# Half-slot order, PSUM banks and layer norms in a four-layer graph network

## The chip, the cores and the metric

The kernel runs on one core of a Trainium2 chip. The metric is the device time of one execution in microseconds (us); lower is better. A core has five engines with instruction streams of their own: TensorE (PE, matmuls; PEld is its weight load), VectorE (DVE), ScalarE (ACT), GpSimd (POOL) and SyncE (SP, which here only issues DMAs). Each engine works its stream in order. They wait for each other through semaphores.

## The reference

Sixteen graphs of 1,024 nodes with 128 features pass through four layers; after each stands a residual sum and a layer norm.

```python
x = layernorm(x + att(x, adj))         # 0: relu(q) relu(k)^T, masked softmax, times v
x = layernorm(x + edge_max(x, adj))    # 1: max over neighbours j of relu(p[i] + q[j] + b)
x = layernorm(x + mlp(x, adj))         # 2: (x + adj^T x) W1, relu, W2
x = layernorm(x + sage3(x, dilate(adj)))  # 3: three convolutions on a thinned adjacency
```

Two parts set the shape of the kernel. Layer 1 takes for each node and each of 128 features a maximum over its neighbours. And `dilate` walks the rows of the adjacency one after the other: in each row with more than ten neighbours some are removed, a removal at (n, m) also removes (m, n), and so earlier rows change what later rows see.

```python
def step(carry, n):
    row = jnp.take(carry, n, axis=0)
    num = jnp.sum(row)
    sf = jnp.where(num > 10, (num + 1) // 2, 1)
    rm = row & (cumsum(row) % sf == 0)    # and only where num > 1
    carry = carry.at[n].set(row & ~rm)
    carry = carry.at[:, n].set(carry[:, n] & ~rm)
```

## The kernel before

**Layer 1 by lookups.** The nodes of a graph are cut into 86 groups of 12, each of two sixes. For every six, `tables_of` (line 447) makes the maximum of q over each of its 64 subsets on VectorE. The neighbours of a node within a six name one subset. So a maximum over neighbours is a lookup by group, written as a matmul with a one-hot matrix, and a running maximum over the 86 groups. One group of one graph is a **slot**; there are 16 x 86 = 1,376 slots. For slot s:

- `count(s, h)` (line 686), two slots ahead: a matmul of the group's adjacency columns with the table `lit` gives `pm` in PSUM, and ScalarE's Relu makes of it the one-hot `hot` (lines 693, 694), for each half h of the 1,024 nodes.
- `table(s)` (line 696), every second slot: two transposes bring the subset table of two groups into PSUM (`pt`), ScalarE copies it to `high` (line 707), and `low_part` (line 710) has VectorE take the difference `low` (line 713), so that two rounded products give the full precision.
- `look_up(s, h, pg)` (line 716): four row-packed matmuls into the two banks of a tile `pg` (line 722).
- the maximum of `best` and `pg` on VectorE (line 782; in a graph's first slot a copy, line 780).

**The other layers as streams.** Everything else is put between these steps. Generators (`scores`, `attend`, `rest`, `tables_of`) yield one piece at a time through `ask` (line 248): its engine, a cost in us, whether it takes or gives back a PSUM bank, a delay in slots since the stream's last piece, and an event that must have happened. `advance(engines)` (line 667) walks through the streams and emits each piece whose engine still has room. The room grows by a fixed amount each slot (`ROOM`, line 660). It is a plan made while the program is written out: no time is measured in it, and the engines then keep the order. `attend` (line 352) is the softmax and the product with v of layer 0 for the next graph; `scores` (line 289) makes q, k, v and the scores, and after layer 0 its q and p for layer 1; `rest` (line 382) finishes layer 1 of the graph before and does layer 2. `columns_of` (line 269) transposes a graph's rows, `product_of` (line 278) multiplies, each into a bank from `shared` (line 251).

**A slot** (`slot`, line 734) writes out: `low_part` in odd slots; pieces on PE, then pieces on ACT, DVE and POOL; both counts of slot s + 2; both lookups; pieces on PE again; due steps of the dilation; in even slots the table; the first maximum; pieces on ACT, DVE and POOL; the second maximum.

**PSUM** has eight banks. `pg` takes two tiles of two banks, `pm` two banks (tag `subset`), the pieces of the streams one (tag `shared`), tables and the dilation's counts one (tag `tables`).

**The layer norms** of layers 0 to 2 are `norm` (line 261): eight `bn_stats` on VectorE, then `norm_rows` (line 206) on GpSimd: ten small operations for mean and factor, and eight `tensor_scalar` that apply them (line 222).

**The dilation** (`dilation`, line 477) runs through 32 blocks of 32 rows, all 16 graphs at once, as one more generator that yields (slots until the next step, VectorE cost, whether the next step wants a bank). A block has 43 slots: a matmul counts each row's remaining neighbours (`pc`, line 553), VectorE copies them (`low_counts`, `rest`, lines 556 to 558); GpSimd walks the 31 rows within the block, eleven small operations a row in a chain (lines 571 to 581), and notes the hits; those go through DRAM and back in another layout (lines 585 to 589); then VectorE takes them out (`hit_T`, line 592) and does the bulk: for each of four groups q two scans (`rank`, line 618), ScalarE's absolute value (line 621), the comparison `gone` (line 624), and a transpose for later blocks (`last_T`, line 629). The results go to DRAM through SP's queue (`removed`, `removed_T`). At the start of the next block the last of them is taken out of its rows and counted (lines 545 to 558).

Ahead of the slots the first graph's attention is computed alone; after them `rest` of the last graph, the last step of the dilation, and layer 3.

Of the kernel before, what the change touches and what calls it, by code (L numbers as in the profile page):

```python
# [29 lines left out]
F32 = mybir.dt.float32  # L30
# [41 lines left out]
def tile_graph_layers(ctx: ExitStack, tc, a, out):  # L72
# [133 lines left out]
    def norm_rows(dst, src, st):  # L206

        mv = small.tile([P, 4, T], F32, name="ln_mv")
        mean, apart, var, rs = (mv[:, i, :] for i in range(4))
        gp = nc.gpsimd  # L210
        gp.tensor_add(mean, st[:, :, 1], st[:, :, 4])
        gp.tensor_sub(apart, st[:, :, 1], st[:, :, 4])
        gp.tensor_scalar(mean, mean, -0.5, 0.0, op0=ALU.mult, op1=ALU.add)
        gp.tensor_mul(apart, apart, apart)
        gp.tensor_add(var, st[:, :, 2], st[:, :, 5])
        gp.tensor_scalar(var, var, 1.0 / D, LN_EPS, op0=ALU.mult, op1=ALU.add)
        gp.tensor_scalar(apart, apart, 0.25, 0.0, op0=ALU.mult, op1=ALU.add)
        gp.tensor_add(var, var, apart)
        gp.tensor_tensor(rs, var, mhalf, op=ALU.pow)
        gp.tensor_mul(mean, mean, rs)  # L220
        for t in range(T):
            gp.tensor_scalar(dst[:, t, :], src[:, t, :], rs[:, t:t + 1], mean[:, t:t + 1],
                             op0=ALU.mult, op1=ALU.add)
# [6 lines left out]
    def layers_012():  # L230
# [15 lines left out]
        happened, streams, made, planned = {}, [], [], False  # L246
# [4 lines left out]
        def shared(name):  # L251
            if planned:
                return psum.tile([P, 512], F32, tag="shared", name=name, bufs=1)
            return psum.tile([P, 512], F32, tag="subset", name=name, bufs=2)

        def tables_bank(name):

            return psum.tile([P, 512], F32, tag="tables", name=name, bufs=1)


        def norm(dst, src):
            st = small.tile([P, T, 6], F32, name="ln_st")
            for t in range(T):
                yield ask("V", 0.29, same=True)
                nc.vector.bn_stats(out=st[:, t, :], in_=src[:, t, :])
            yield ask("Pool", 0)
            norm_rows(dst, src, st)
# [21 lines left out]
        def scores(b):  # L289
# [48 lines left out]
            yield ask("A", 0.01, after=("X1", b), delay=5)  # L338
# [43 lines left out]
        def rest(b):  # L382
# [16 lines left out]
            yield from columns_of(xT, X[b], first=5)  # L399
            left = w4.tile([P, T, D], F32, name="left", tag="y")  # L400
            parts = w4.tile([P, 3, T, D], BF, name="parts")
            for k in range(3):
                yield ask("A", 1.05)
                nc.scalar.copy(parts[:, k], left if k else X[b])
                if k < 2:
                    yield ask("V", 1.22)
                    nc.vector.tensor_sub(left, left if k else X[b], parts[:, k])
# [69 lines left out]
        def dilation():  # L477
# [59 lines left out]
            now, last_T = load(0), None  # L537
            for _ in prepare(0, *now):
                pass
            for k in range(K):  # L540
                E, V, _, counts = now
# [8 lines left out]
                p = tables_bank("pc")  # L550
                for c, slots in enumerate(((0, 2, 3), (1, 4))):
                    for i in slots:
                        nc.tensor.matmul(p[:B, c * R:(c + 1) * R], spread[:, i].rearrange("p q g -> p (q g)"), of_row,
                                         start=(i == slots[0]), stop=(i == slots[-1]))
                low = dil.tile([B, R], F32, name="low_counts")
                nc.vector.tensor_copy(low, p[:B, 0:R])
                rest = dil.tile([B, R], F32, name="rest")
                nc.vector.scalar_tensor_tensor(rest, p[:B, R:2 * R], 0.5, half_mask[:, own], op0=ALU.add, op1=ALU.mult)  # L558
                if k + 1 < K:
# [4 lines left out]
                for n in range(R - 1):  # L564
# [17 lines left out]
                    yield 0.95, 0.06, False  # L582
# [7 lines left out]
                yield B * NP / K - 37.75, 0, False  # L590
# [24 lines left out]
                for q in range(Q):  # L615
                    rank = dil.tile([P, N], F32, name="rank", bufs=2)
                    for h, s in enumerate(halves):
                        nc.vector.tensor_tensor_scan(rank[:, s], E[:, q, s], E[:, q, s], rank[:, 511:512] if h else 0.0,  # L618
                                                     op0=ALU.add, op1=ALU.max)
                        yield 0.34, 1.2, False  # L620
                    nc.scalar.activation(rank, rank, AF.Abs, bias=centre[:, q:q + 1], scale=scale[:, q:q + 1])  # L621
                    yield 0.34, 0, False
                    gone = dil.tile([P, N], BF, name="gone", bufs=2)
                    nc.vector.scalar_tensor_tensor(gone, rank, width[:, q:q + 1], E[:, q, :],  # L624
                                                   op0=ALU.is_equal, op1=ALU.mult)
                    nc.sync.dma_start(out=removed[k, :, q, :], in_=gone)
                    yield 0.34, 1.3, False
                    if after:
                        nc.vector.transpose(last_T[:, q].rearrange("p k r -> p (k r)"), gone[:, (k + 1) * R:])
                        if after > 1:  # L630
                            nc.sync.dma_start(out=removed_T[k + 2:, :, q, own].rearrange("k p r -> p k r"),
                                              in_=last_T[:, q, 1:, :])
                    yield 0.34, 0.8, q == Q - 1
                if after:
                    now = following
# [19 lines left out]
        now, bank_free = 0, 0  # L655
# [10 lines left out]

        def advance(engines):
            nonlocal bank_free
            for stream in list(streams):
                while True:  # L670
# [5 lines left out]
                    if (engine not in engines or now < at + delay or room[engine] <= 0 and give is False or (take and now < bank_free)  # L676
                            or after and now <= happened.get(after, now) or third and now % 3):
                        break
                    room[engine] -= cost
                    if take:  # L680
                        bank_free = 1 << 30
                    if give:
                        bank_free = now + 0.5
# [12 lines left out]
        def table(s):  # L696
# [4 lines left out]
            pt = tables_bank("pt")[:, :2 * P]  # L701
# [32 lines left out]
        def slot(s, last):  # L734
# [19 lines left out]
            advance(("PE",))  # L754
            advance(("A", "V", "Pool"))
            ahead = s + 2 if s + 2 < last else None
            if ahead is not None:
                for h in range(2):
                    count(ahead, h)
            pgs = []  # L760
            if s >= 0:
                for h in range(2):
                    pgs.append(psum.tile([P, 2, 512], F32, tag="wide", name="pg", bufs=2))
                    look_up(s, h, pgs[h])
                hots.pop(s)
            now = s + 0.5
            advance(("PE",))
            if s >= 0:
                while due <= s and (s % 2 or not wants_bank):
                    after, cost, wants_bank = next(dilate, (B * NP, 0, False))  # L770
                    due += after
                    room["V"] -= cost
            if ahead is not None and ahead % 2 == 0:
                table(ahead)
            for h, pg in enumerate(pgs):
                if h:
                    advance(("A", "V", "Pool"))
                own = bests[b][:, :, halves[h]]
                if g == 0:
                    nc.vector.tensor_copy(own, pg)  # L780
                else:
                    nc.vector.tensor_max(own, own, pg)  # L782

        dilate = dilation()
        due, wants_bank = 0.0, True
# [16 lines left out]
        with tc.manual_schedule(engines={mybir.EngineType.PE, mybir.EngineType.Activation, mybir.EngineType.DVE,  # L802
                                         mybir.EngineType.Pool}):
            planned = True
# [3 lines left out]
            planned = False  # L808
# [312 lines left out]
```

## Time and profile before

| what | value |
|---|---|
| median of three runs | 7495.03 us (7492.15 to 7495.25) |
| span of the profiled execution | 7491.3 us |
| mean granted clock of TensorE | 0.844 |
| busy: PE, DVE, ACT, POOL | 5627.2, 5493.4, 3343.2, 3585.3 us |
| slots, from the first maximum to the last | 132.3 to 6166.1 us |
| maximum at line 782 | 2,720 times, 1,211 ns each |
| `hot` at line 694 | 2,752 times, 686 ns each |
| norm applied on GpSimd, line 222 | 384 times in layers 0 to 2, 450 ns each |
| subtraction `left`, line 407 | 32 times, about 1.22 us each |

The profile is one execution, recorded by the hardware. A "busy" time is the sum of the instructions of an engine; matmuls are pipelined[...], so a busy PE is not PE at its peak. A wait names the engine and line that waited, and whose end released it. A window is a stretch of the span in us from its start. Durations in the prediction are means of such rows.

### The profile page before, as it was taken

To read this page: it belongs to the slowest core of one execution; us is meant where nothing else is said; L and a number is where in the kernel's file an instruction comes from. 1 tells how busy PE (TensorE), PEld (TensorE's weight loads), DVE (VectorE), ACT (ScalarE), POOL (GpSimd) and SP (SyncE) were. 2 spreads that over 40 slices of the span, in tenths; PEclk is the share of its full clock that TensorE was granted. 3 is DMA by queue.
4 is the path that set the end of the run, shared out by engine and by line. 5 is a ranking of instruction groups with operands and counts; after the bars stand their busy time and mean duration, and the time that the engine had idled before them with its cause. 6 is when DMAs were issued, how large, how long until landed. Compare 5 with 4: busy or idle time off the path is not lost.

```text
span 7491.3 us, 84114 instructions
## 1 busy us (share of the span) xinstructions
PE 5627.2 (75%) x26430; PEld 2905.1 (39%) x26554; DVE 5493.4 (73%) x8459; ACT 3343.2 (45%) x5465; POOL 3585.3 (48%) x11637
## 2 busy tenths in 40 slices
PE   6768687878787777676767676777777767778996
PEld 3334243434343434343334343433343324555653
DVE  3788787878788878787878777878787883444453
ACT  3445454445454545454444444445444432333751
POOL 3454555555555555555554555555555541110116
PEclk8889787878787979787878788888888778888998
DMA  5121212121212121212121202121111106665544
GB/s 34 18 24 18 29 18 29 18 29 18 28 18 29 19 29 19 28 18 29 18 29 18 28 14 28 15 28 18 28 16 21 22 18 112 113 113 110 186 161 152
DMA packets 494372, 318.87 MB, mean 43 GB/s; under 512 B 316650, under 2 KB 445668, under 8 KB 489828
## 3 DMA queue, kind: packets, MB, share of 16 engines
q0 software_dynamic: 105648, 84.20, 12.9%
q1 hardware_dynamic: 383600, 228.10, 10.7%
q8 instruction: 209, 3.42, 0.2%
q10 hardware_dynamic: 4676, 1.19, 0.1%
q14 instruction: 239, 1.96, 0.1%
HBM read 413.70 MB, written 118.16 MB: 71 GB/s over the span
## 4 chain that ended last, share of the span: by engine, by line
DVE 30%; PE 29%; POOL 22%; issue 8%; ACT 6%; DMA 4%; SPq 0%; another core or an unknown queue 0%; DVEq 0%; ACTq 0%; POOLq 0%
DVE best L782 13%; PE pg L722 7%; PE pagg L901 5%; DVE rank L618 3%; PE pav L373 3%; POOL sc L576 2%; PE pm L693 2%; DVE sub L463 2%; POOL hit L578 2%; DVE gone L624 2%; POOL sc L571 2%; POOL last_rank L579 2%; POOL sc L573 2%; PE pe L363 2%; PE psc L325 2%
## 5 line engine op out<-in xcount | busy, mean ns | idle before, releaser
L782 DVE TENSOR_TENSOR best<-best,pg 128x1024 f32<-128x1024 f32 x2720 | 3207.4, 1211 | 704.6 <-PE pg L722 701.5
L694 ACT ACTIVATE hot<-pm,one_less 128x512 fp32r<-128x512 f32 x2752 | 1739.2, 686 | 1059.5 <-PE pm L693 1056.4
L722 PE MATMUL pg<-hot,high 64*128 64x512 f32 x5504 | 1485.8, 536 | 911.6 <-DVE best L782 888.4
L722 PEld LDWEIGHTS pg<-hot,high 64*128 64x128 f32 x5504 | 583.5, 208 | 2068.7 <-DVE best L782 1595.5
L722 PE MATMUL pg<-hot,low 64*128 64x512 f32 x5504 | 1229.0, 442 | 0.0
L693 PE MATMUL pm<-AT,lit 120*128 120x512 fp8e4 x2752 | 955.9, 431 | 13.2 <-ACT hot L694 6.0
L487 POOL DMA_DIRECT2D E<-in_adj_dram x128 | 70.3, 558 | 1844.2 <-issue 1028.4
L707 ACT CAST high<-pt 128x256 fp32r<-128x256 f32 x688 | 255.1, 371 | 935.0 <-PE pt L705 933.1
L722 PEld LDWEIGHTS pg<-hot,low 64*128 64x128 f32 x5504 | 612.1, 218 | 30.8
L571 POOL TENSOR_SCALAR sc<-low_counts,half_mask,rest 16x1 f32<-16x1 f32 x992 | 341.3, 344 | 287.7 <-DVE rest L558 191.1
L576 POOL TENSOR_SCALAR sc<-sc 16x1 f32<-16x1 f32 x992 | 394.6, 398 | 104.4
L693 PEld LDWEIGHTS <-lit 120*128 120x128 fp8e4 x2752 | 271.1, 107 | 323.8 <-issue 260.3
L573 POOL TENSOR_SCALAR sc<-sc 16x1 f32<-16x1 f32 x992 | 331.8, 334 | 107.2
L621 ACT ACTIVATE rank<-rank,centre,scale 128x1024 f32<-128x1024 f32 x128 | 158.6, 1239 | 502.0 <-DVE rank L618 502.0
L373 PE MATMUL pav<-v,eT 128*128 128x128 f32 x2048 | 330.7, 317 | 52.4 <-ACT eT L366 52.3
L325 PE MATMUL psc<-kT,qT 128*128 128x512 f32 x512 | 291.9, 653 | 83.5 <-DVE y L377 48.5
L578 POOL TENSOR_SCALAR hit<-V,sc 16x31 bf16<-16x31 bf16 (+30 forms) x992 | 354.5, 357 | 0.0
L931 POOL TENSOR_TENSOR length<-length,mhalf 128x8 f32<-128x8 f32 x48 | 79.0, 1645 | 570.3 <-DVE length L930 570.3
L579 POOL TENSOR_SCALAR last_rank<-V,sc 16x31 f32<-16x31 bf16 (+30 forms) x992 | 344.4, 347 | 0.0
L373 PEld LDWEIGHTS pav<-v,eT 128*128 128x128 f32 x2048 | 290.5, 222 | 124.7 <-ACT eT L366 75.9
L705 PE MATMUL pt<-ident,sub 128*128 128x128 f32 x1376 | 322.0, 320 | 1.7
L363 PE MATMUL pe<-ident,e 128*128 128x128 f32 x1024 | 212.0, 344 | 146.9 <-ACT e L335 88.7
(242 smaller groups left out, 9213.5 us busy)
## 6 DMA issues: line engine op xcount, KB each, us to landing
removed<-gone SPq DMA_DIRECT2D x128, 256.0 KB
An<-in_adj_dram POOLq DMA_DIRECT2D x16, 1024.0 KB, 15.8
E<-in_adj_dram POOLq DMA_DIRECT2D x128, 128.0 KB, 6.4
gone_all<-removed POOLq DMA_DIRECT2D x64, 256.0 KB, 12.1
near<-in_adjT_dram POOLq DMA_DIRECT2D x16, 1024.0 KB, 17.3
h<-x SPq DMA_DIRECT2D x32, 512.0 KB
kept<-near SPq DMA_DIRECT2D x16, 1024.0 KB
share<-share SPq DMA_DIRECT2D x32, 512.0 KB
```

The costliest lines, as they stand in the source:

```text
L325: nc.tensor.matmul(psc, qT[:, t * P:(t + 1) * P], kT[:, s], start=True, stop=False)
L373: nc.tensor.matmul(pav, eT[:, c, :], values[b][:, c, :], start=(c == 0), stop=(c == T - 1))
L571: gp.tensor_scalar(half, mine, half_mask[:, m], rest[:, n:n + 1], op0=ALU.mult, op1=ALU.add)
L573: gp.tensor_scalar(sf, half, 5.5, sf, op0=ALU.is_gt, op1=ALU.mult)
L576: gp.tensor_scalar(to, at, sf, none, op0=ALU.subtract, op1=ALU.subtract)
L578: gp.tensor_scalar(hit[:, n, n + 1:], V[:, n, n + 1:], at, None, op0=ALU.is_equal)
L579: gp.tensor_scalar(last[:, n + 1:], V[:, n, n + 1:], to, None, op0=ALU.is_le)
L693: nc.tensor.matmul(pm, lit[:, r, :], AT[b * (T + 1) + c][:, halves[h]], start=True, stop=True)
L694: nc.scalar.activation(hots[s][:, halves[h]], pm, AF.Relu, bias=one_less)
L722: nc.tensor.matmul(pg[:, a], part[rows, at * P:(at + 1) * P], hots[s][rows, halves[h]], start=(k == 0), stop=(k == 1))
L782: nc.vector.tensor_max(own, own, pg)
L901: nc.tensor.matmul(pa[:, s], piece[:, c, :], m[c][:, s], start=(c == 0 and k == 0), stop=(c == T - 1 and k == 1))
```

## The change

- In each half slot the lookup now stands first, then the pieces (PE, then the others). The dilation's steps come in the first half, the two counts and the table in the second, and each half ends with its maximum.
- `shared` has two banks, and `advance` keeps account of which piece holds which. The tag `tables` is gone: tables take turns with the counts on the two `subset` banks, and the dilation's counts take a bank of `shared` through `hold`.
- `norm_rows` is split: `norm_factors` stays on GpSimd; for layers 0 to 2 the eight applications become ScalarE activations, asked for four slots after GpSimd's part. The last norm, of layer 3, still uses `norm_rows` on GpSimd.
- The two subtractions `left` in `rest` go from VectorE to GpSimd, and ScalarE's copies after them are asked for 2.5 slots later.
- Two delays of five slots (transposes after a norm) become half a slot.
- In the dilation the scans of group q stand ahead of the comparison of group q - 1, `low_counts` and `rest` are a step of their own after the counts' matmul, and the slots of a block are divided anew: rows every 0.90 in place of 0.95, 7.34 in place of 5.25 for the way through DRAM, steps of the bulk every 0.36 in place of 0.34.

```diff
     def norm_rows(dst, src, st):
+        rs, mean = norm_factors(st)
+        for t in range(T):
+            nc.gpsimd.tensor_scalar(dst[:, t, :], src[:, t, :], rs[:, t:t + 1], mean[:, t:t + 1],
+                                    op0=ALU.mult, op1=ALU.add)
+
+    def norm_factors(st):
...
-        for t in range(T):
-            gp.tensor_scalar(dst[:, t, :], src[:, t, :], rs[:, t:t + 1], mean[:, t:t + 1],
-                             op0=ALU.mult, op1=ALU.add)
+        return rs, mean
...
         def shared(name):
-            if planned:
-                return psum.tile([P, 512], F32, tag="shared", name=name, bufs=1)
-            return psum.tile([P, 512], F32, tag="subset", name=name, bufs=2)
+            return psum.tile([P, 512], F32, tag="shared", name=name, bufs=2)
...
             yield ask("Pool", 0)
-            norm_rows(dst, src, st)
+            rs, mean = norm_factors(st)
+            for t in range(T):
+                yield ask("A", 0.25, same=(t > 0), delay=4)
+                nc.scalar.activation(dst[:, t, :], src[:, t, :], AF.Identity, bias=mean[:, t:t + 1],
+                                     scale=rs[:, t:t + 1])
...
-            yield ask("A", 0.01, after=("X1", b), delay=5)
+            yield ask("A", 0.01, after=("X1", b), delay=0.5)
...
-            yield from columns_of(xT, X[b], first=5)
+            yield from columns_of(xT, X[b])
...
-                yield ask("A", 1.05)
+                yield ask("A", 1.05, delay=2.5 if k else 0.5)
                 nc.scalar.copy(parts[:, k], left if k else X[b])
                 if k < 2:
-                    yield ask("V", 1.22)
-                    nc.vector.tensor_sub(left, left if k else X[b], parts[:, k])
+                    yield ask("Pool", 0)
+                    nc.gpsimd.tensor_sub(left, left if k else X[b], parts[:, k])
...
-                p = tables_bank("pc")
+                yield 0, 0.3, True
+                p = shared("pc")
+                own_bank = hold()
...
+                yield 0.5, 0.2, False
                 low = dil.tile([B, R], F32, name="low_counts")
...
-                    yield 0.95, 0.06, False
+                    yield 0.9, 0.06, False
...
-                yield B * NP / K - 37.75, 0, False
+                yield B * NP / K - 35.66, 0, False
...
+                for q in range(Q + 1):
+                    if q < Q:
+                        rank = ranks[q] = dil.tile([P, N], F32, name="rank", bufs=2)
...
+                    if q:
+                        gone = dil.tile([P, N], BF, name="gone", bufs=2)
...
...
-            pt = tables_bank("pt")[:, :2 * P]
+            pt = psum.tile([P, 512], F32, tag="subset", name="pt", bufs=2)[:, :2 * P]
...
+            for h in range(2):
+                now = s + 0.5 * h
+                if s >= 0:
+                    pg = psum.tile([P, 2, 512], F32, tag="wide", name="pg", bufs=2)
+                    look_up(s, h, pg)
+                advance(("PE",))
+                advance(("A", "V", "Pool"))
+                if h == 0:
+                    while s >= 0 and due <= s and not (wants_bank and taken >= 2 and given.get(taken - 2, 1e9) > now):
+                        after, cost, wants_bank = next(dilate, (B * NP, 0, False))
+                        due += after
+                        room["V"] -= cost
+                elif s + 2 < last:
+                    for half in range(2):
+                        count(s + 2, half)
+                    if s % 2 == 0:
+                        table(s + 2)
+                if s >= 0:
+                    own = bests[b][:, :, halves[h]]
...
```

## The prediction

> **What bounds the kernel now.** First the page's busy shares: no engine is full (PE 75%, DVE 73%, ACT 45%, POOL 48%), so the time lies in waits between engines. Then the view by line: the maximum at line 782 (2,752 with its 32 copies at line 780, two per slot) starts at 132.3 us and ends at 6166.1 us. That is 1,376 slots of 4.385 us, 86 slots (about 381 us in the middle) a graph, and all that the change touches, but for a few steps before and after.
>
> Then the waits, us in total, times, longest:
>
> ```profile
> DVE best L782 <- PE pg L722: 701.5, 340, 18.0
> PE pg L722 <- DVE best L782: 888.4, 989, 26.0
> ACT xT L276 <- POOL X L222: 228.2, 16, 19.8
> DVE hit_T L592 <- DMA hit_p<-hit: 129.7, 16, 23.5
> DVE gone L624 <- ACT rank L621: 77.9, 46, 3.5
> DVE low_counts L556 <- PE pc L553: 56.3, 30, 3.6
> ```
>
> The reader is to see that VectorE waits for lookups and TensorE for VectorE, in turn. Sixteen times, once a graph, PE and ACT stand still for a layer norm that GpSimd has not applied; sixteen times VectorE waits for the dilation's result.
>
> A graph holds two dilation blocks (43 slots each), so I cut one graph at the dilation's own marks: from its row counts (line 558) to VectorE's first step on the result (line 592), the "window" in which GpSimd walks 31 rows; and from there to the next counts, the "bulk". The view by stretches (length; busy us of PE, PEld, DVE, ACT, POOL with instructions; clock; DMA):
>
> ```profile
> 2400.80:2542.40 141.60, 113.76 (x570) 59.81 (x575) 113.47 (x179) 75.66 (x131) 95.92 (x332) 0.92 0.07 7
> 2542.40:2587.00 44.60, 30.06 (x148) 14.82 (x147) 39.96 (x56) 19.24 (x29) 1.83 (x4) 0.89 0.20 41
> 2587.00:2724.20 137.20, 107.51 (x533) 51.04 (x532) 107.18 (x162) 65.95 (x119) 105.60 (x356) 0.90 0.20 23
> 2724.20:2776.20 52.00, 30.51 (x108) 13.22 (x108) 47.19 (x67) 16.70 (x25) 2.32 (x5) 0.51 0.36 53
> ```
>
> The two bulks are VectorE's (40 of 44.6, 47 of 52.0). In the first window nobody is full: GpSimd's rows end at 2517.2, 25 us before the result is used, and VectorE idles 28 us. The second window ends on GpSimd: rows end at 2712.3, the DMA lands, VectorE has waited 7.9 us. So the windows have different limits: coupling in the first, GpSimd's chain in the second.
>
> **What the Trainium skill says.** "TensorE: Matmul & The Clock Gate" (Part 1, What's actually happening): the clock is half or full, by recent activity. The trace agrees: 0.51 in the second bulk, about 0.9 in the windows. I assume the same clock after; 0.05 more or less is 6% of PE's 282 us, 17 us a graph, perhaps half of it on the path. "Perfetto Trace Analysis" (Optimization Strategy): repeated bubbles can mean too few PSUM buffers. Here one bank serves all of the other layers' pieces, and all eight are in use (4 lookups, 2 counts, 1 tables, 1 pieces). "PSUM — Partial Sum Buffer" (bank collisions): guard by bank, so a table written into a counts bank must wait until ScalarE has read that bank; no trace of before has this wait.
>
> **The change, part by part.** Sums are per graph.
>
> 1. *Order in the half slot.* Before, PE does pieces, counts, both lookups, pieces, table; VectorE gets nothing new between one slot's second lookup and the next slot's first. After, one lookup opens each half slot. Nothing is added: 8 lookup matmuls and 2 maxima a slot as before. What can be won is VectorE's 701.5/16 = 44 us, less about 11 that belong to the stall in 2.
>
> 2. *Norms applied on ScalarE, four slots after GpSimd's factors.* GpSimd loses 3 x 8 x 0.45 = 10.8 us (line 222): 3.5 in the first window, 7 in the second (bn_stats of one and two norms lie there in the changed order). ScalarE gains 24 instructions. "ScalarE: Activation LUTs" (What ACT_TABLE_LOAD costs) gives 280 ns + 0.833 ns an element with one pointer operand, 93 for a second, 93 overlapped: about 0.39 us, 9.4 us a graph. The rank activation (two pointers, 1,024 elements) took 1,239 ns, formula 1,226. ScalarE has room, busy 177.6 of 375.4. The new waits: behind a norm on ACT stand the `hot` activations, two slots ahead of the lookups, so some 6 us late are covered. The 228.2 us wait goes.
>
> 3. *The two subtractions of line 407 go to GpSimd*: VectorE loses 2 x 1.22 = 2.4 us. No row shows such a subtraction there; "GPSIMD Engine Reference" (Elementwise) has 4,497 ns for 2,048 elements, so I estimate 2.25 us for 1,024. Bounds: 1.2 (VectorE's) to 4.5. In the changed order the first falls into the bulk, where GpSimd is idle, the second at the start of the second window's rows: +2.25 there.
>
> 4. *Two banks for pieces; tables share the two counts banks.* Gain: a piece no longer waits for the last eviction (in the waits `psc <- y`, 48.5 us in all; small). Cost: in each even slot the order is count, count, table on two banks, so the table's transposes wait for the first `hot`. One such place, before:
>
> ```profile
> 2268.22 0.60 PE L693 MATMUL pm<-AT,lit 120*128 120x512 fp8e4 x2
> 2268.65 1.27 ACT L694 ACTIVATE hot<-pm,one_less 128x512 fp32r<-128x512 f32 x2 [0.40 <-PE pm L693]
> ```
>
> The first hot ends 0.43 + 0.69 = 1.1 us after the counts start; the counts occupy PE for 0.45. PE waits 0.65 us if ScalarE is free, about 1.2 if an eviction (0.59) stands before it, 0 where VectorE is behind anyway. I take 0.65 for 43 tables: 28 us, some 12 in each window. Behind the table on PE stands the next lookup, and VectorE behind that.
>
> 5. *Dilation.* Scan of row group q before gone of q-1 hides ScalarE's rank: 77.9/16 = 4.9 us off, in the bulks. Counts are read a slot after their matmul: 56.3/16 = 3.5 off as a wait, given back as a later start. The writes of `gone` and `last_T` on SP's queue move along, some 2.5 us later for each of the first three; they are read a block later, and the next that VectorE waits for on SP, the result's, is a window away. The counts' matmul now takes a pieces bank, so it stands behind an eviction of at most 0.7 us. By the changed order the slots are, first window, bulk, second window, bulk: 34.0, 8.0, 35.7, 8.3 before, 36.0, 6.6, 36.3, 7.1 after. A slot's two maxima (2.35 us back to back) move with them.
>
> *Sum.* First window: PE 113.8 + two more slots (3.8 at full clock) + 12 for tables + 3.4 of today's waits on ACT's results = 133; VectorE 113.5 + 4.7 - 2.4 = 116, with half of its 28 us idle 130; GpSimd 112.9 + about 11 for the DMA = 124. I take 133. Second window: GpSimd 137.2 - 7 + 2.25 = 132.4 stands above VectorE (109 busy) and PE (107.5 + 5 moved in + 12); I take 133: the stall and the wait on the result go only as far as that chain. Bulks: 40.0 - 1.4 x 2.35 + 1.8 = 38.5; 47.2 - 1.2 x 2.35 + 4.1 = 48.5. Together 353 against 375.4, 6.0% less. Fifteen graphs (132 to 5843 us) lose 0.06 x 5711 = 341 us; the last, where VectorE waits for GpSimd already (23.5 us), about 5; outside the slots a norm and two subtractions change engines, +1. Span 7491.3 - 345 = 7146; the runs' median is 3.7 above the span: **7150 us**.
>
> **The rivals.**
>
> - *Coupling vanishes.* GpSimd bounds both windows (124, 132.4), bulks at VectorE's 37 and 45: 338, ten per cent less, 7495 - 570 = about 6930. For: VectorE is busy for 308 of 375 us only. Against: the table's wait.
> - *Only small gain.* The table's wait eats the first window's gain (141), the second is GpSimd's (134), bulks 41 and 50: 366, or 2.5% less: about 7340. For: PE busy 114 of 141.6 leaves 28 us for all waits.
> - *Slower: tables wait behind ScalarE.* PE is busy 282 us a graph; its other waits, 93.5 less 52 for VectorE's maxima, are 41.5. 375.4 - 282 - 41.5 = 52 us is all that 43 tables may cost: from 1.2 us each PE sets a longer graph. ScalarE's pieces (0.6 to 1.35 us) and bursts of norms stand before `hot` in the same half slot. At 1.5 us: +13 a graph, +206: 7700. Against: not every half slot has a piece, and part of the 41.5 goes with item 1.
> - *The change does nothing*: the order is written out by hand, so it does move instructions; only an exact offset gives this.
>
> **How the numbers follow.** Forecast (7010 to 7240) 0.53; coupling vanishes 0.13; small gain 0.25; slower 0.07; no difference 0.02. Range 6990 to 7340: it leaves out most of the first rival, the last two and a little of the second. A measurement of this kernel tells about 0.2% from no change. Faster by more than 0.2%: 0.91; within: 0.02; slower: 0.07.
>
> **What would show it.** Right: the wait of `xT` on GpSimd's X is gone, `best <- pg` falls from 701.5 to some 400, `gone <- rank` below 20; `hit_T` keeps a wait in the second windows; a new wait of `pt` on `hot`, some 0.65 us each; first windows near 133 us, second near 133. Wrong: first windows still 141 (the table's wait is larger), second windows well under 132 (rows got faster), a clock that moved by over 0.05, or `hot` waiting for GpSimd's factors on ACT.

## The result, and the profile after

| | median us | runs | ratio to before, 95% interval |
|---|---|---|---|
| before | 7495.14 | 4, 7492.15 to 7509.31 | |
| after | 7411.32 | 4, 7408.36 to 7422.13 | 0.9887 [0.987, 0.9904] |

The change makes the kernel 1.1% faster. The forecast was 4.6%; the time lies 71 us above the range's upper end.

The page of the kernel after gives busy time and share by engine, and the shares of the chain that ended last:

```profile
PE 5789.6 (78%) x26554; PEld 2790.6 (38%) x26554; DVE 5516.8 (74%) x8427; ACT 3510.6 (47%) x5849; POOL 3475.9 (47%) x11285
...
PE 48%; DVE 31%; ACT 10%; issue 5%; POOL 4%; DMA 2%; ACTq 0%; DVEq 0%; SPq 0%; POOLq 0%
```

The chain of the kernel before:

```profile
DVE 30%; PE 29%; POOL 22%; issue 8%; ACT 6%; DMA 4%; SPq 0%; another core or an unknown queue 0%; DVEq 0%; ACTq 0%; POOLq 0%
```

GpSimd has all but left the path, but PE and ScalarE took its place. The view of waits says at what (us in total, times, longest):

```profile
PE pg L737 <- DVE best L791: 609.5, 685, 11.0
...
PE pt L720 <- ACT hot L709: 463.7, 655, 5.1
...
DVE low L728 <- ACT high L722: 364.6, 364, 7.0
...
DVE best L791 <- PE pg L737: 255.5, 293, 4.2
...
DVE e L330 <- PE psc L328: 172.0, 161, 15.4
...
DVE y L379 <- PE pav L375: 122.2, 98, 5.1
```

Three of these waits, in the kernel before:

```profile
DVE y L377 <- PE pav L373: 57.5, 60, 5.5
...
DVE e L328 <- PE psc L326: 43.5, 49, 15.3
...
DVE low L713 <- ACT high L707: 33.7, 51, 6.0
```

Here `e` and `y` are VectorE's steps on the scores and on the product with v. VectorE's wait for lookups fell from 701.5 to 255.5 us, and PE's wait for the maxima from 888.4 to 609.5. The stall of `xT` on X, 228.2, is no longer in the list. New are 464 us in which PE stands before a table; the wait of VectorE for that table's copy grew from 34 to 365.

The same graph as in the prediction, cut at the same marks, in the view by stretches (length; busy us of PE, PEld, DVE, ACT, POOL with instructions; clock; DMA):

```profile
2400.20:2540.90 140.70, 120.19 (x604) 56.85 (x600) 114.21 (x180) 80.38 (x143) 91.96 (x324) 0.96 0.07 7
2540.90:2583.90 43.00, 26.33 (x114) 11.53 (x112) 38.91 (x56) 17.92 (x27) 4.50 (x6) 0.75 0.27 47
2583.90:2726.80 142.90, 121.00 (x560) 52.74 (x556) 111.04 (x162) 73.54 (x136) 100.99 (x339) 0.90 0.15 19
2726.80:2775.20 48.40, 25.38 (x94) 10.29 (x96) 45.16 (x68) 15.98 (x23) 2.32 (x5) 0.56 0.48 64
```

Both windows are over 140 us; the forecast was 133. In both PE is busy for 120 us, and the next table shows that the rest of PE's time is two waits.

Means over the 12 graphs of blocks 4 to 27, cut like this, from the instructions of each trace (us; "table" is PE's idle time before `pt`, "lookup" before `pg`, mostly for the maximum that empties the bank):

| window, kernel | length | PE busy | table | lookup | other idle |
|---|---|---|---|---|---|
| first, before | 142.5 | 115.7 | 0 | 12.0 | 14.8 |
| first, after | 139.2 | 118.4 | 11.3 | 9.4 | 0.1 |
| first, counts split (below) | 129.9 | 116.5 | 0 | 13.3 | 0.1 |
| second, before | 137.0 | 103.3 | 0 | 10.8 | 22.9 |
| second, after | 142.4 | 120.9 | 12.3 | 9.0 | 0.2 |
| second, counts split | 133.6 | 120.0 | 0.8 | 11.6 | 1.2 |

One such place, an even slot of the kernel after (start, length, engine and operation, and in brackets the idle time before it and what ended it):

```profile
2423.30 0.60 PE L708 MATMUL pm<-AT,lit 120*128 120x512 fp8e4 x2
...
2423.78 1.27 ACT L709 ACTIVATE hot<-pm,one_less 128x512 fp32r<-128x512 f32 x2 [0.98 <-PE pm L708]
...
2424.52 0.44 PE L720 MATMUL pt<-ident,sub 128*128 128x128 f32 x2 [0.62 <-ACT hot L709]
...
2424.89 0.50 PE L737 MATMUL pg<-hot,high 64*128 64x512 f32 x2
...
2424.99 0.37 ACT L722 CAST high<-pt 128x256 fp32r<-128x256 f32 x1
...
2425.40 0.42 DVE L728 TENSOR_TENSOR low<-pt,high 128x256 fp32r<-128x256 f32 x1
```

Both counts fill the two banks; the table's transposes `pt` then stand on PE until ScalarE has made the first `hot` (0.62 us), and the next slot's lookup, already allowed to run, starts only behind them. `high` comes behind the second `hot`, and VectorE's `low` behind `high`.

### The profile page after: what moved, and what is told of

It reads as the page before. It is cut to its first block, busy times and chain, and to the rows that moved or that the text cites. A ratio compares the mean times of both kernels' runs of the same rounds, so it can differ in the third digit from the quotient of the medians.

```text
span 7420.3 us, 84498 instructions
## 1 busy us (share of the span) xinstructions
PE 5789.6 (78%) x26554; PEld 2790.6 (38%) x26554; DVE 5516.8 (74%) x8427; ACT 3510.6 (47%) x5849; POOL 3475.9 (47%) x11285
## 3 DMA queue, kind: packets, MB, share of 16 engines
q1 hardware_dynamic: 383600, 228.10, 10.9%
## 4 chain that ended last, share of the span: by engine, by line
PE 48%; DVE 31%; ACT 10%; issue 5%; POOL 4%; DMA 2%; ACTq 0%; DVEq 0%; SPq 0%; POOLq 0%
PE pg L737 15%; DVE best L791 13%; ACT hot L709 6%; PE pagg L910 5%; PE pm L708 4%; DVE rank L626 4%; PE pav L375 3%; PE psc L327 3%; PE pp L284 2%; PE pa L417 2%; PE pt L720 2%; DVE sub L465 2%; DVE gone L632 2%; PE pe L365 2%; PE py L438 1%
## 5 line engine op out<-in xcount | busy, mean ns | idle before, releaser
L791 DVE TENSOR_TENSOR best<-best,pg 128x1024 f32<-128x1024 f32 x2720 | 3226.8, 1212 | 266.3 <-PE pg L737 255.5
L737 PE MATMUL pg<-hot,high 64*128 64x512 f32 x5504 | 1528.6, 549 | 689.2 <-DVE best L791 609.5
L737 PE MATMUL pg<-hot,low 64*128 64x512 f32 x5504 | 1247.6, 445 | 0.0
L720 PE MATMUL pt<-ident,sub 128*128 128x128 f32 x1376 | 337.3, 331 | 482.5 <-ACT hot L709 463.7
L728 DVE TENSOR_TENSOR low<-pt,high 128x256 fp32r<-128x256 f32 x688 | 289.9, 421 | 368.6 <-ACT high L722 364.6
L720 PEld LDWEIGHTS pt<-ident,sub 128*128 128x128 f32 x1376 | 151.2, 154 | 877.2 <-ACT hot L709 875.6
L582 POOL TENSOR_SCALAR sc<-sc 16x1 f32<-16x1 f32 x992 | 391.9, 395 | 104.7
L708 PEld LDWEIGHTS <-lit 120*128 120x128 fp8e4 x2752 | 200.6, 101 | 518.4 <-issue 500.0
L579 POOL TENSOR_SCALAR sc<-sc 16x1 f32<-16x1 f32 x992 | 318.8, 321 | 107.5
L409 POOL TENSOR_TENSOR left<-X,parts 128x1024 f32<-128x1024 f32 x16 | 34.1, 2133 | 674.3 <-ACT parts L406 674.3
L465 DVE TENSOR_TENSOR sub<-sub,q 128x24 f32<-128x24 f32 (+11 forms) x768 | 316.4, 413 | 23.8 <-ACT q L287 10.5
## 6 DMA issues: line engine op xcount, KB each, us to landing
An<-in_adj_dram POOLq DMA_DIRECT2D x16, 1024.0 KB, 14.8
gone_all<-removed POOLq DMA_DIRECT2D x64, 256.0 KB, 12.3
```

The lines of the kernel that those rows point to most:

```text
L465: nc.vector.tensor_max(sub[:, :n_g, n:2 * n], sub[:, :n_g, 0:n], qg[:, 2 * g0:2 * g0 + n_g, k:k + 1].to_broadcast([P, n_g, n]))
L582: gp.tensor_scalar(to, at, sf, none, op0=ALU.subtract, op1=ALU.subtract)
L708: nc.tensor.matmul(pm, lit[:, r, :], AT[b * (T + 1) + c][:, halves[h]], start=True, stop=True)
L720: nc.tensor.transpose(pt[:, k * P:(k + 1) * P], subs[b, g0][:, g - g0 + k, :], ident)
L737: nc.tensor.matmul(pg[:, a], part[rows, at * P:(at + 1) * P], hots[s][rows, halves[h]], start=(k == 0), stop=(k == 1))
```

## The experiments

The theory: the new wait on PE before the tables, in PE's own order, is what ate the gain, because a lookup stands behind each table. The rivals: VectorE's wait of `low` for `high`, which comes of the same place and is not much shorter, is what costs; the order of the half slot as such (a maximum now stands behind pieces) costs; or the norms or the subtractions, moved between engines, cost. All ratios are to the kernel before. It was run again with each set of experiments, with medians of 7495 to 7502 us, so a difference between runs of two sets is uncertain by some 6 us.

| edit | median us | ratio, 95% interval |
|---|---|---|
| e1: counts split over the half slots | 7129.51 | 0.9502 [0.9482, 0.9523] |
| e2: e1, `low` later | 7156.68 | 0.9541 [0.9521, 0.9561] |
| e3: e1, each maximum ahead of VectorE's pieces | 7025.09 | 0.9368 [0.9346, 0.9391] |
| e4: after, with the banks of before | 7230.08 | 0.9638 [0.9619, 0.9657] |
| e5: after, with the order of before | 7163.04 | 0.9556 [0.9541, 0.9571] |
| e6: before, with the norms on ScalarE | 7209.87 | 0.9624 [0.9609, 0.9638] |
| e7: after, with the norms on GpSimd | 7635.49 | 1.0195 [1.0179, 1.0212] |
| e8: after, subtractions on VectorE | 7351.68 | 0.9809 [0.9792, 0.9825] |
| e9: after, `low` later | 7467.57 | 0.9955 [0.9938, 0.9971] |
| e10: e1, subtractions on VectorE | 7152.32 | 0.9526 [0.9512, 0.954] |
| e11: e3, subtractions on VectorE | 7059.41 | 0.9405 [0.9389, 0.9421] |
| e12: e11, table in the first half slot | 7086.99 | 0.944 [0.9426, 0.9454] |

### e1: the counts split, so that the table finds its bank empty

```diff
-                elif s + 2 < last:
-                    for half in range(2):
-                        count(s + 2, half)
-                    if s % 2 == 0:
-                        table(s + 2)
+                if s + 2 < last:
+                    count(s + 2, h)
+                    if h and s % 2 == 0:
+                        table(s + 2)
```

The same instructions run; the first count now stands half a slot ahead of the table that takes its bank.

> The changed kernel with one count in each half slot (count of half h in half h) in place of both in the second; the table still stands last in the second half of even slots. The table's bank is then the one of the first half's count, which ScalarE has read long before. Theory 'chain count, hot, table, high, low': the wait of pt on hot (464 us on PE, 876 on its weight load) falls under 100 us, the wait of low on high (365 us) to about half, and the time falls by 150 to 300 us, to 7110 to 7260. Rival 'pieces in front of the maxima and separate maxima' (VectorE is held by its own pieces, which wait for PE in the same half slot): pt's wait falls too, but VectorE idles elsewhere instead; the time moves by less than 60 us.

7129.51 us, 282 less than after. The waits of this kernel:

```profile
PE pg L737 <- DVE best L790: 721.9, 665, 17.4
...
DVE best L790 <- PE pg L737: 226.4, 299, 3.6
DVE low L728 <- ACT high L722: 187.4, 170, 6.2
...
DVE e L330 <- PE psc L328: 146.6, 172, 15.7
...
PE pt L720 <- ACT hot L709: 78.2, 72, 5.1
```

PE's wait of `pt` for `hot` falls from 464 to 78 us. The windows are 129.9 and 133.6 us (table above), 9 less each, with nearly the same busy PE and the same granted clock (0.97 and 0.90, for 0.96 and 0.90). So a wait of 0.71 us in some 43 places per graph was worth 18.6 us a graph, two thirds of its own sum (29); much of the rest came back as a longer wait for the maxima. But VectorE's wait for `high` was halved by the same edit; e9 and e4 bear on which of the two counts.

### e2 and e9: VectorE's wait of low for high, made shorter alone

`low_part(s + 1)` of odd slots goes from the slot's start to right before its first maximum; e9 does this to the kernel after, e2 to e1.

```diff
-            if s % 2 and s + 1 < last:
-                low_part(s + 1)
             for h in range(2):
...
+                if h == 0 and s % 2 and s + 1 < last:
+                    low_part(s + 1)
                 if s >= 0:
                     own = bests[b][:, :, halves[h]]
```

> The changed kernel with VectorE's low of odd slots after the pieces, right before the first maximum, in place of first in the slot; the counts and the table stay together, so pt still waits for hot. If VectorE's wait for high (365 us, not in the forecast's sum) is what costs: that wait falls under 150 us and the time by 100 to 250 us. If PE's wait for hot (the 0.65 us that the forecast took) is what costs: pt's wait stays near 464 us and the time within 50 us of 7411.

> As e1, and VectorE's low of odd slots stands after the pieces, right before the first maximum, in place of first in the slot. Chain theory: the wait of low on high falls under 100 us and the time is 40 to 120 us below e1. Rival: the time is within 30 us of e1, since VectorE then waits for something else.

e9 took 7467.57 us, 56 more than after. Its waits:

```profile
PE pt L720 <- ACT hot L709: 465.0, 655, 5.1
...
DVE low L728 <- ACT high L722: 202.6, 206, 7.5
...
PEld L708 <- DVE low L728: 133.6, 94, 4.0
```

VectorE's wait fell by 162 us, PE's wait for the table stayed within 1.3 us, and the time rose: the later `low` frees the table's bank later, and the next count waits for that. e2 is 27 us slower than e1 for the same edit. So the first rival finds no support. It isn't excluded by this pair: the edit takes away less than half of the wait, and brings a new one.

### e4 and e5: the banks and the order of before, each put back alone

e4 gives the tables their own bank again, and the pieces one, which the dilation's counts share. e5 keeps the new banks, and writes a slot out as before: both counts, both lookups, then the table.

```diff
...
-            return psum.tile([P, 512], F32, tag="shared", name=name, bufs=2)
+            if planned:
+                return psum.tile([P, 512], F32, tag="shared", name=name, bufs=1)
+            return psum.tile([P, 512], F32, tag="subset", name=name, bufs=2)
...
-            pt = psum.tile([P, 512], F32, tag="subset", name="pt", bufs=2)[:, :2 * P]
+            pt = psum.tile([P, 512], F32, tag="tables", name="pt", bufs=1)[:, :2 * P]
...
```

```diff
...
+            advance(("PE",))
+            advance(("A", "V", "Pool"))
+            ahead = s + 2 if s + 2 < last else None
+            if ahead is not None:
+                for h in range(2):
+                    count(ahead, h)
+            pgs = []
+            if s >= 0:
+                for h in range(2):
+                    pgs.append(psum.tile([P, 2, 512], F32, tag="wide", name="pg", bufs=2))
+                    look_up(s, h, pgs[h])
+            now = s + 0.5
+            advance(("PE",))
...
+            if ahead is not None and ahead % 2 == 0:
+                table(ahead)
+            for h, pg in enumerate(pgs):
+                if h:
+                    advance(("A", "V", "Pool"))
...
```

> The changed kernel with the banks of before: one bank for tables alone, one for the pieces, also for the dilation's counts; order of the half slot, norms, subtractions and dilation as changed. Chain theory: pt no longer waits for hot, low's wait on high falls under 150 us, the time falls by 100 to 250 us unless pieces on one bank give it back. Rival 'two banks of pieces are needed with lookups first': waits of PE pieces on evictions (psc on e, pp on z, ptr on xT) grow by over 300 us and the time is at or above 7411.

> The changed kernel with the half-slot order of before (pieces, both counts, both lookups, pieces, dilation, table, first maximum, pieces, second maximum); banks, norms, subtractions and dilation as changed. Chain theory: here a table stands a whole pair of lookups behind the counts, so its wait for hot on the counts' bank is gone (pt on hot under 50 us) and the lookups wait as before; time 7250 to 7380, that is: the new order as written gave back more than it won. Rival 'the order is what the change won': slower than 7411, about 7450, since best on pg goes back to some 700 us.

e4 took 7230.08 us. The waits of e4:

```profile
PE pg L739 <- DVE best L793: 987.8, 980, 13.4
...
DVE low L730 <- ACT high L724: 380.7, 356, 10.4
...
DVE best L793 <- PE pg L739: 113.9, 143, 3.1
```

VectorE still waits 381 us for `high`, where under 150 was expected, and yet 181 us are gone; no wait of `pt` for `hot` is left in the view. This is a second removal of that wait, by other means than e1, and it has the same sign though it gives up the second bank for pieces. So the gain isn't VectorE's wait for `high`.

But e4 doesn't price the wait. In the windows of the 12 graphs PE stands idle nearly as long as in the kernel after (19.4 and 20.6 us, for 20.8 and 21.5), since its idle time before lookups grew: 15.6 us for 9.4, and 20.1 for 9.0. Shorter is the time for which its matmuls count as busy, above all in the second window. Here is that window of e4 for the graph shown above, where the kernel after has 121.00 us for as many matmuls, at a clock of 0.90:

```profile
2502.00:2634.60 132.60, 112.08 (x560) 51.24 (x556) 110.37 (x162) 72.22 (x136) 101.12 (x339) 0.96 0.15 17
```

How much of the 181 us belongs to the wait and how much to the higher clock isn't shown.

e5 took 7163.04 us. The waits of e5:

```profile
DVE best L795 <- PE pg L737: 635.2, 642, 6.9
...
PE pm L708 <- ACT hot L709: 336.4, 340, 5.3
...
PE pm L708 <- DVE low L728: 181.4, 147, 3.9
```

With the old order the shared banks make the counts wait instead (336 and 181 us), and VectorE waits for lookups nearly as before (635 for 701); still it beats the kernel after by 248 us, and took less than was expected of it. So the order of the half slot as written, with both counts just ahead of the table, lost 248 us; the same order with the counts split (e1) wins 33 over e5. The fault is one place in the order. What the order is worth without it isn't priced by these 33 us, for e5 has a fault of its own, the 518 us for which its counts wait.

### e6 and e7: the norms

e6 puts into the kernel before only the split of `norm_rows`, the eight ScalarE applications and the two shorter delays; e7 takes only these out of the kernel after. Of e6's edit:

```diff
...
             yield ask("Pool", 0)
-            norm_rows(dst, src, st)
+            rs, mean = norm_factors(st)
+            for t in range(T):
+                yield ask("A", 0.25, same=(t > 0), delay=4)
+                nc.scalar.activation(dst[:, t, :], src[:, t, :], AF.Identity, bias=mean[:, t:t + 1],
+                                     scale=rs[:, t:t + 1])
...
```

> The kernel before with the norms of layers 0 to 2 applied on ScalarE and the delays that go with it, nothing else. Stall theory: the wait of xT on GpSimd's X (228 us) is gone and of that 60 to 130 us come off the time (7365 to 7435), the rest is taken up by GpSimd's rows in the second windows, where the wait of hit_T stays. Rival: the rows bind the whole second window, the wait on hit_T grows by what the stall gave, and the time is within 30 us of 7495.

> The changed kernel with the norms applied on GpSimd again, delays of before, all else as changed. Stall theory: 50 to 130 us slower than 7411. Rival: within 30 us, since in the changed kernel VectorE and PE lose that time at the tables anyway.

e6 took 7209.87 us: the norms with their delays, which weren't tried apart, are alone worth 285 us, more than was expected and more than the whole change. The second window of one of its graphs, by stretches:

```profile
2500.90:2630.00 129.10, 109.73 (x553) 53.48 (x554) 110.19 (x165) 69.79 (x127) 100.84 (x338) 0.93 0.14 13
```

Over 12 graphs it is 126.5 us, against 137.0 before. e7, with 7635.49 us, is slower than the kernel before. Its waits for norms that GpSimd applies (first of `xT` on ACT, then of its transposes on PE) are longer than the 228 and 180 us of before:

```profile
ACT xT L274 <- POOL X L209: 419.0, 15, 32.2
PE ptr L272 <- POOL X L209: 378.6, 17, 28.1
```

So the norms did not cost: without them the rest of the change is a loss of 2%, and in the kernel after they are worth 224 us.

### e8, e10, e11: the subtractions

```diff
-                yield ask("A", 1.05, delay=2.5 if k else 0.5)
+                yield ask("A", 1.05)
...
-                    yield ask("Pool", 0)
-                    nc.gpsimd.tensor_sub(left, left if k else X[b], parts[:, k])
+                    yield ask("V", 1.22)
+                    nc.vector.tensor_sub(left, left if k else X[b], parts[:, k])
```

> The changed kernel with the two subtractions of rest on VectorE again, without the longer delay of ScalarE's copies. If VectorE's work is what counts: 32 x 1.22 = 39 us, so 20 to 50 us slower. If GpSimd's standing still for ScalarE's parts (675 us, 16 times) or its 2.1 us each in the rows is what counts: 0 to 60 us faster.

> As e1 (counts split), with the two subtractions on VectorE as in e8. If e8's gain of 60 us is GpSimd's time in the second windows: 40 to 90 us below 7130, the second window shorter by 3 us or more. If it belonged to the table's wait: within 25 us of 7130.

> As e3 (counts split, maxima ahead of VectorE's pieces), with the two subtractions on VectorE. e3 waits 4.9 us for hit_T in each second window, so GpSimd's rows bind there: without the subtractions on GpSimd that window shrinks by 3 to 5 us and the time falls 40 to 80 us below 7025. If VectorE binds: 0 to 40 us slower.

The row of the first of them in the kernel after:

```profile
L409 POOL TENSOR_TENSOR left<-X,parts 128x1024 f32<-128x1024 f32 x16 | 34.1, 2133 | 674.3 <-ACT parts L406 674.3
```

One takes 2.13 us on GpSimd, for 1.22 on VectorE in e8. The part has both signs. In the kernel after, giving the subtractions back to VectorE wins 60 us (7351.68). With the counts split (e10 for e1) the median is 23 us higher (by the ratios 18 us, with intervals that overlap), within the 25 expected if e8's gain belonged to the table's wait; with the maxima first as well (e11 for e3) it is 34 higher, as expected if VectorE's work is the limit there. In e8 GpSimd's rows in the second window take 116.1 us in place of 122.6, though nobody waited for them in the kernel after. In e3 VectorE does wait for the dilation's result there, 4.9 us a window; e11 takes that wait away, and the window still grows from 132.2 to 134.5 us. Which chain turns the sign wasn't found.

### e3 and e12: on from e1

e3 is e1 with each half's maximum ahead of VectorE's pieces and of the dilation's steps.

```diff
                 advance(("PE",))
-                advance(("A", "V", "Pool"))
-                if h == 0:
-                    while s >= 0 and due <= s and not (wants_bank and taken >= 2 and given.get(taken - 2, 1e9) > now):
+                advance(("A", "Pool"))
                 if s + 2 < last:
                     count(s + 2, h)
...
                         nc.vector.tensor_max(own, own, pg)
+                advance(("V", "A", "Pool"))
+                if h == 0:
+                    while s >= 0 and due <= s and not (wants_bank and taken >= 2 and given.get(taken - 2, 1e9) > now):
```

e12 is e11 with the table ahead of the count in the first half of even slots, and `low_part` behind that half's maximum.

```diff
                 if s + 2 < last:
-                    count(s + 2, h)
-                    if h and s % 2 == 0:
+                    if h == 0 and s % 2 == 0:
                         table(s + 2)
+                    count(s + 2, h)
...
+                if h == 0 and s % 2 == 0 and s + 2 < last:
+                    low_part(s + 2)
                 advance(("V", "A", "Pool"))
```

> As e1, and in each half slot VectorE's maximum stands ahead of VectorE's pieces and of the dilation's steps, which follow it. Chain theory: little beyond e1, within 60 us of it. Rival: the waits of e on psc (172 us), y on pav (122) and hT on pa (61) fall to under a third, maxima are no later than their lookups, and the time is 150 us or more below e1.

> As e11, with the table in the first half of even slots ahead of the first count, and low right after that half's maximum. The waits of low on high (272 us in e3) and of pt on hot fall under 60 us each. If those waits still cost: 60 to 150 us below e11, 6850 to 6920. If the other waits take their place (pm on low, since the table's bank is now held until low): within 40 us of e11.

e3 took 7025.09 us, 104 less than e1: the fastest here, 6.3% below before and 5.2% below after. Its waits, and then those of e12:

```profile
PE pg L737 <- DVE best L785: 567.3, 369, 19.6
...
DVE low L728 <- ACT high L722: 271.5, 272, 9.2
...
DVE best L785 <- PE pg L737: 201.3, 332, 2.4
```

```profile
DVE best L783 <- PE pg L737: 380.7, 442, 10.6
...
PE pm L708 <- ACT hot L709: 267.8, 209, 10.2
...
DVE low L728 <- ACT high L722: 202.6, 301, 1.8
```

In e3 PE waits 155 us less for maxima, since a lookup's banks are emptied before the pieces are worked. The gain lies between the two expectations, so the second rival has a share: the maximum behind pieces cost 104 us, beside the 282 of the counts. In e12 the wait only moves, from the table to the counts behind it (268 us); VectorE's wait for `high` stays at 203 us, where under 60 was expected, and 28 us are lost against e11.

## Why the prediction was wrong in size

The direction held, and the new wait was named and sized; how it adds to the other waits was wrong. By terms, against its sum: the slots take 5,949 us (136.9 to 6086.0) where 5,688 was forecast, +261. Outside the slots it is +13.7 in place of +1. The runs' median lies 9 below the profiled span, not 3.7 above. 261 + 13 - 13 is the miss of 261 us. Within a graph, forecast against the means of the 12 graphs: first window +6, first bulk +5, second window +9, second bulk 0. (The forecast was worked out on one graph of 375.4 us; the mean of the 12 before is 381.2.)

**The step that failed is the sum over a window**: "PE 113.8 + two more slots (3.8 at full clock) + 12 for tables + 3.4 of today's waits on ACT's results = 133; VectorE 113.5 + 4.7 - 2.4 = 116, with half of its 28 us idle 130", and then the larger of the two. Its terms were good: PE's work came to 118.4 (117.6 forecast), the tables' waits to 11.3 (12), the estimated 0.65 us each to 463.7/655 = 0.71. Part of that fit is luck: the estimate has the two counts on PE for 0.45 us and `hot` done after 1.1, where the slot shown above has 0.60 and starts `pt` after 1.22; the two differences nearly cancel. The 3.4 of waits on ACT's results went, to 0.1. Two things were left out.

- PE went on waiting before lookups, mostly for the maxima: 9.4 us in the first window, 9.0 in the second. The sum struck that wait out, as if VectorE, taken at 130, ran beside PE at 133. But the two work in turn through two `pg` tiles: while PE stands before a table no lookup or piece is made, VectorE comes later to its maxima, and afterwards PE waits for these. VectorE's own idle time in the first window, 25.4 us, is 10.5 for `high`, 6.7 for the scores, 3.9 for `y` and only 1.8 for lookups; in the second it is 31.2, of which 14.0 for lookups and 10.6 for `high`. The table's wait came mostly on top: with it away (e1) the windows are 9 us shorter each, and PE's wait for maxima is still there, at 13.3 and 11.6.
- The second window was given to GpSimd at 132.4. It isn't GpSimd's. After the change GpSimd's rows end 19.7 us before the result is used (10.9 before, when VectorE waited 7 for it), and e6, which has no subtraction on GpSimd, runs the same window in 126.5, where the forecast's terms give 137.2 - 7 = 130.2. PE has the longest sum: 120.9 busy where 112.5 was forecast, + 12.3 + 9.0 = 142.2 of 142.4. 557 matmuls fall into it and not 511; 32 of the 46 more are `pa`, which take 12.3 us for 3.9.

By its numbered steps:

1. *Order*: VectorE's wait for lookups fell to 255.5, further than the 400 forecast. But all of these 446 us came back as longer waits for `high` (34 to 365), for the scores (44 to 172) and for `y` (58 to 122). The order as written cost 248 us (e5). The forecast counted half of VectorE's idle time as gained; one wait that falls was no such gain.
2. *Norms*: right in kind, too small. The stall went as forecast, GpSimd's second rows fell from 126.0 to 117.2 us in e6 (8.8; 7 forecast), but the graph gained 21 us (381.2 to 360.0). The forecast let the window go only to GpSimd's floor, which was set too high. One application took 162.2/384 = 0.42 us of ScalarE's busy time (487 ns from start to end, overlapping its neighbours), near the 0.39 estimated from the Trainium skill, "ScalarE: Activation LUTs" (What ACT_TABLE_LOAD costs).
3. *Subtractions*: the price held (2.25 us estimated from the Trainium skill, "GPSIMD Engine Reference" (Elementwise), 2.13 measured), the sign didn't: the move cost 60 us there (e8). Some 6 of these lie after the slots, by one profile of each: from the last maximum to the end it is 1,334 us after, 1,328 in e8 and in e7, 1,325 before. Subtractions and norms together were costed at +1 there.
4. *Banks*: the wait was named and sized rightly, its effect not. The Trainium skill, "PSUM — Partial Sum Buffer" (PSUM bank collisions raise a hardware error), says to guard by bank; the guard is the wait seen here, 0.71 us a time. The second bank for pieces was called small; e1 with it is 100 us faster than e4 without it, though those two differ in the counts' place too.
5. *Dilation*: `gone` on `rank` fell from 77.9 to nothing, as said. The second bulk came to 48.5 us, as forecast, though of its sum the last 4.1 is not derived. The first came to 43.7 for 38.5. The graph that was cut is not a typical one: its first bulk is the shortest of the twelve before (44.9 by these marks; the mean is 49.3). The mean fell by 5.6, where 6.1 was forecast. In e5 it falls further, to 39.4, so the half-slot order holds some 4 us. PE's wait before tables (3.2 there) seems not to be what does it, for e4 has no such wait and 43.2; the cause stays open.

Of the rivals, "only small gain" named the table's wait as the cause, with windows of 141 and 134; the second was wrong there as well. "Slower" put its point at 1.2 us a table, and that wasn't reached (0.71). The mean granted clock moved by 0.012 (0.844 to 0.856), in the change's favour.

The change's parts from the runs, added in this order: norms on ScalarE -285 (e6), banks, dilation and subtractions in the old order -47 (e5 less e6), the half-slot order as written +248: 7411. Added in another order the parts differ. The order's fault in one place is worth -282 (e1), the maxima's place -104 more (e3).

## What to carry to other kernels

Where two engines hand work to each other through few buffers, don't count on the other's spare time to hide a new wait on one of them. Here about two thirds of it came off the time when it was removed (e1). So the safe sum is that engine's busy time, plus the new wait, plus its wait for the partner, and the maximum is taken only against engines outside the pair. When tiles of two kinds take turns on the same banks, ask at each allocation who emptied that bank and how long ago, and put other work between the two. Before a change of several parts is priced, price each alone: here one part held more than the whole gain. And work the sum out on the mean of many rounds: a single one may be an odd one, as the first bulk was here.

## What the runs showed beside that

- VectorE's busy time rose from 5493.4 to 5516.8 us although 32 subtractions (39 us) had left it. The maxima (+19) and the small maxima of `tables_of` (301.8 to 316.4) hold 34 of the 62 us (23 + 39) that are to be explained. By starts in the traces, two maxima back to back step by 1.13 us, where one alone takes 1.21.
- The same 26,554 matmuls kept PE busy for 5789.6 us after and 5667.2 in e3, at nearly the same mean clock (0.856 and 0.860). (Before it was 5627.2, but the trace has only 26,430 of them.) So a forecast of PE's busy time from another order can be off by some per cent.
